# Half of a residual added by a gathering DMA, one bias addition moved to GpSimd, and two of eight steps with centre and gate in one matmul

## The chip, the core and the metric

The kernel runs on one core of a Trainium2 chip. Its time is the device time of one launch in microseconds; several runs are taken, and their median is the figure that counts. A profile is one further execution, recorded by the hardware profiler.

The engines are named as in the profile: PE is TensorE's matmul and PEld its weight load, DVE is VectorE, ACT is ScalarE, POOL is GpSimd, and SP is SyncE, which here only issues transfers. Each engine works through its own queue in order.

## The reference

The input `x` has 512 x 512 positions of 64 channels. Two layers are added to it, each to a group-normalized copy of its input:

```
x = x + L0(gn(x))            # triangle multiplication
x = x + L1(gn(x))            # 12 x 12 Fourier modes, mixed over channels
```

The first layer, cut to what matters here:

```
xn    = layernorm(x)
left  = (xn @ left_w + left_b)   * mask * sigmoid(xn @ lgate_w + lgate_b)
right = (xn @ right_w + right_b) * mask * sigmoid(xn @ rgate_w + rgate_b)
gate  = sigmoid(xn @ ogate_w + ogate_b)
out   = einsum('bkjd,bkid->bijd', left, right)
out   = layernorm(out) @ out_w + out_b
return out * gate
```

`mask` is 1 where both row and column are marked. About half of the 512 rows are, so `out` before the layernorm is zero at most positions.

## The kernel before

**Stages.** At most 256 rows are marked here, and the function `compact` packs these rows and columns. One after the other it takes statistics of `x` (to about 200 us of the profile), makes `left` and `right` (to 450), multiplies them channel by channel (to 620), computes `u` = layernorm(`out`) @ `out_w` + `out_b` for the marked positions (to about 750), runs the **output stage** (to about 1450) and, last, adds the Fourier layer and stores the result. The whole loop of the `u` steps and the output stage is one Python loop over steps `s`, which issues every engine's instructions in a hand-written order (`tc.manual_schedule`). The tile library adds only the waits between them.

**Steps and units.** Eight steps make a unit, `k, n = divmod(s, SIZE)`. The first 8 units are the `u` steps (`k < first`); the other 32 are the output stage, numbered `v = k - first`. A unit is a chunk of 32 columns times one half of the ranked rows. Its `x` is gathered as two transfers (`load`, r = 0 and 1) of 128 partitions x 32 positions x 64 channels, 1 MB each, into one of five buffers, `x_of(v)`, within the big tile `places`. For every second unit the rows are marked ones and `u` comes from memory by 32 transfers of `load_u`; for the others `u` is one constant row, `rows_of["out"]`.

**What a step does.** At step `s` the matmul engine transposes step `s + 13` (`t_ps`, line 1038), multiplies step `s` by the gate weights (`w_ps`, line 1045 through `times`) and step `s + 12` by the centring matrix (`c_ps`, the same line). ScalarE turns the transposed block into `xt_c` (line 1040), and squares the centred block (line 1076). VectorE sums the squares of two steps (line 1083), scales a step's gate product by the reciprocal root of the variance (line 1274) and, after each second step, adds the gate's bias to the part `z` of 16 positions (line 1280). A unit thus has four parts, c = 0 to 3. Each then goes through a sigmoid on ScalarE (line 1221), a product with `u` on GpSimd (`gated`, line 1109) and an addition to `x` on GpSimd (`added`, line 1113).

The root is taken once per unit, at step 5 of the unit before (`root`, line 1089). It needs another function table than the sigmoid, so two table loads stand around it.

**What is done with the sum.** `transform` (line 1140) multiplies the finished halves by a row basis: the half r = 0 at step 0 of the next unit, r = 1 at step 4. `statistics` (line 1168) takes VectorE's statistics of the finished unit four channel pairs a step, from step 3 of the next unit on. `store` writes a half to memory from SyncE: r = 0 at step 7 of its own unit, r = 1 at step 3 of the next. On the same queue `load_u` is issued at step 4 of each even unit. Every fourth unit the statistics are joined (`join_means`, `join_squares`, `join_rest`); after every second unit `save` copies the transform out of PSUM on ScalarE.

**Order within a unit, before.** Sigmoids stand at the even steps, products at the odd steps and additions at the even ones: part c has its sigmoid at step 2 + 2c, its product at 3 + 2c, its addition at 4 + 2c, counted on into the next unit. The gathers for unit `v + 3` stand behind the product at step 3 and behind the addition at step 6 on GpSimd's queue. PSUM holds two banks for `c_ps`, two for `w_ps`, two for `t_ps`, one for sums and biases (`scratch`) and one for the transform.

Of the kernel before, what the change touches and what calls it, by code (L numbers as in the profile page):

```python
# [9 lines left out]
F32 = mybir.dt.float32  # L10
# [36 lines left out]
def conv_preact_kernel(ctx: ExitStack, tc: tile.TileContext, t: dict):  # L47
# [573 lines left out]
    def compact(fc):  # L621
# [15 lines left out]
        def gather(dst, src, idx, r, jc):  # L637
            nc.gpsimd.indirect_dma_start(  # L638
                out=dst, out_offset=None, in_=src, in_offset=bass.IndirectOffsetOnAxis(ap=idx[:, r, jc : jc + 1], axis=0)
            )  # L640
# [190 lines left out]
        with tc.tile_pool(name="tri", bufs=1) as trp:  # L831
# [92 lines left out]
            with tc.manual_schedule(), tc.tile_pool(name="late", bufs=1) as lp:  # L924
# [65 lines left out]
                with tc.tile_pool(name="np_x", bufs=LEAD + 2) as tp, tc.tile_pool(name="np_q", bufs=2) as sqp, tc.tile_pool(  # L990
# [6 lines left out]
                    ps_c = ps_w = None  # L997

# [43 lines left out]
                    def times(pool, name, s, w):  # L1042
                        ps = pool.tile([P, 8, C], F32, name=name)
                        for i in range(4):
                            nc.tensor.matmul(ps[:, 2 * i : 2 * i + 2, :], xts[s][:, i, :], w, start=True, stop=True)  # L1045
                        return ps

                    def centered(s):
                        if s >= first * SIZE:
                            return times(ps_c, "c_ps", s, center_x)  # L1050

                        ps = ps_y.tile([P, 2, 4, P], F32, name="y_ps")
# [12 lines left out]

                    def of_pair(t, e):

                        return t.rearrange("p (h e i) c -> p h e i c", h=2, e=2)[:, :, e]

                    def squared(s, cps):  # L1070
                        n = s % SIZE
                        if n % 2 == 0:
                            sqs[s // 2] = sqp.tile([P, 16, C], F32, name="sq_c")
                        sq = sqs[s // 2][:, 8 * (n % 2) : 8 * (n % 2) + 8, :]
                        if s >= first * SIZE:
                            nc.scalar.activation(sq, cps, AF.Square)  # L1076
# [14 lines left out]
                    def load(k, r):  # L1091
                        jc, half = units[k]
                        gather(
                            x_of(k)[:, r * JC : (r + 1) * JC].rearrange("p j c -> p (j c)"), tiles, src_i, 2 * half + r, jc
                        )
# [6 lines left out]
                    def gated(k, c):  # L1102
# [6 lines left out]
                        nc.gpsimd.tensor_mul(zs[k, c], zs[k, c], u)  # L1109
# [5 lines left out]
                    def finished():  # L1115

                        z = zs.pop((last, 3))
                        made = [ps_c.tile([P, 8, C], F32, name="c_ps") for _ in range(2)]
# [74 lines left out]
                    for s in range(-LEAD, total_g + 2 * SIZE):  # L1193
# [12 lines left out]
                        if s + LEAD - 1 == first * SIZE:  # L1206
                            products.close()
                            ps_c = products.enter_context(tc.tile_pool(name="np_c", bufs=2, space=PSUM))
                            ps_w = products.enter_context(tc.tile_pool(name="np_w", bufs=2, space=PSUM))
                        if 0 <= s < total_g:  # L1210
                            wps = raw(s) if k < first else times(ps_w, "w_ps", s, gate_x)
                            del xts[s]
                        if 0 <= s + LEAD - 1 < total_g:
                            cps = centered(s + LEAD - 1)
                        if n in (0, 4) and held(1):
                            transform(v - 1, n // 4)

                        if n % 2 == 0:
                            i, c = (0, n // 2 - 1) if n >= 2 else (1, 3)
# [11 lines left out]
                        if n % 2 == 1:  # L1231
                            i, c = (0, (n - 3) // 2) if n >= 3 else (1, 3)
# [4 lines left out]
                        else:  # L1237
                            i, c = (0, (n - 4) // 2) if n >= 4 else (1, 2 + n // 2)
                            if held(i) and (v - i, c) != (last, 3):
                                added(v - i, c)  # L1240
# [21 lines left out]
                        if n == 7 and k + 1 in rss:  # L1262
                            nc.vector.reciprocal(factors[(k + 1) % 2] if k + 1 < first else rss[k + 1], rss[k + 1])
                        if wps is not None:
# [7 lines left out]
                            else:  # L1272
                                rs = rss[k][:, 8 * n : 8 * n + 8].unsqueeze(2).to_broadcast([P, 8, C])
                                nc.vector.tensor_mul(z[:, 8 * odd : 8 * odd + 8, :], wps, rs)  # L1274
                            if odd:
# [3 lines left out]
                                else:  # L1279
# [6 lines left out]
                                else:  # L1286
                                    zs[v, c] = z

                        if n == 7 and held(0) and v < last:
                            store(v, 0)  # L1290
# [243 lines left out]
```

## Time and profile before

| | |
|---|---|
| median of three runs | 1774.15 us (1771.41 to 1779.44) |
| the profiled execution, its own time | 1777.78 us |
| its span, first to last instruction | 1776.0 us |
| TensorE busy, share of the span | 1567.8 us, 88% |
| VectorE busy | 1413.7 us, 80% |
| ScalarE busy | 933.0 us, 53% |
| GpSimd busy | 936.5 us, 53% |
| moved by DMA | 518.48 MB, mean 292 GB/s |
| bias addition of the gate, VectorE, line 1280 | 128 of 1221 ns |
| scaling of the gate product, VectorE, line 1274 | 256 of 672 ns |
| product with `u`, GpSimd, line 1109 | 127 of about 2372 ns |
| addition to `x`, GpSimd, line 1113 | 127 of 2372 ns |
| gather of half a unit, GpSimd's issue, line 638 | 64 of 982 ns |

The shares are means over stages with different limits, so the output stage has to be read by itself. Busy times in the profile are unions of an engine's spans; instructions of one engine overlap a little, so the interval from one start to the next can be shorter than the duration. "Idle before, by X" in a row names the instruction whose end released the waiting one. A gather's landing time is counted from its issue on GpSimd to the arrival of its data.

### The profile page before, as it was taken

The page shows a single profiled execution, that of the slowest core. Times are in us where ns is not written, and L with a number is a line of the kernel's source. Part 1 is how long each engine was busy: PE and PEld are TensorE (multiplying, and loading weights), DVE is VectorE, ACT ScalarE, POOL GpSimd, SP SyncE. Part 2 cuts the span into 40 slices and gives each one's busy share as a digit, 9 for nine tenths or more (in the row PEclk, how much of TensorE's full clock was granted, in tenths as well). Part 3 has the DMA queues.
Part 4 walks back from the last instruction along what each step waited for, and adds up shares of the span by engine and source line. Part 5 has one row for each costly group of instructions (what it writes and reads, how often), then busy time and mean ns, then how long its engine had stood idle before and what let it go on. Part 6 is the DMA issues. An engine that isn't in the chain of part 4 may idle for free. (4 is left out here: it accounts for less than half of the span.)

```text
span 1776.0 us, 32619 instructions
## 1 busy us (share of the span) xinstructions
PE 1567.8 (88%) x10918; PEld 1242.0 (70%) x10918; DVE 1413.7 (80%) x2982; ACT 933.0 (53%) x1660; POOL 936.5 (53%) x695
## 2 busy tenths in 40 slices
PE   6779799997999978899999999999999977998772
PEld 5667666662899867787888888888888745665341
DVE  7989678887455568688999999999999984865451
ACT  3666566663333266676777777777777742011000
POOL 4666211111000037698999999999999881111110
PEclk9999999999899999899999999999999976555555
DMA  7999278878898789868767767776776699999999
GB/s 281 386 386 388 107 206 227 229 229 245 279 305 303 257 246 347 298 196 296 265 242 257 253 233 259 264 249 239 249 264 244 212 318 400 425 427 427 426 427 385
DMA packets 192593, 518.48 MB, mean 292 GB/s; under 512 B 37664, under 2 KB 104480, under 8 KB 151456
## 3 DMA queue, kind: packets, MB, share of 16 engines
q1 hardware_dynamic: 156112, 295.65, 47.5%
q0 software_dynamic: 32832, 218.45, 33.4%
q10 hardware_dynamic: 3472, 2.20, 0.5%
q8 instruction: 89, 1.46, 0.3%
q14 instruction: 88, 0.72, 0.1%
HBM read 311.60 MB, written 204.60 MB: 291 GB/s over the span
## 5 line engine op out<-in xcount | busy, mean ns | idle before, releaser
L1045 PE MATMUL w_ps<-gate_x,xt_c 128*128 128x128 f32 x2048 | 280.5, 281 | 30.0 <-DVE z_t L1274 28.6
L1113 POOL TENSOR_TENSOR places<-places,z_t 128x1024 f32<-128x1024 f32 x127 | 301.3, 2372 | 8.0
L1045 PEld LDWEIGHTS w_ps<-gate_x,xt_c 128*128 128x128 f32 x2048 | 252.0, 194 | 46.4 <-DVE z_t L1274 44.6
L1045 PE MATMUL c_ps<-center_x,xt_c 128*128 128x128 f32 x2048 | 277.0, 279 | 0.8 <-ACT xt_c L1040 0.4
L1045 PEld LDWEIGHTS c_ps<-center_x,xt_c 128*128 128x128 f32 x2048 | 252.8, 194 | 3.8 <-ACT xt_c L1040 3.0
L1440 PE MATMUL l_ps<-places,rinv 24*128 24x512 f32 x512 | 206.2, 1118 | 29.3 <-DVE places L1447 19.0
L1168 DVE BATCH_NORM_STATS2 stats2c<-places 128x6 f32<-128x128 f32 x1024 | 220.5, 278 | 9.9 <-POOL places L1113 9.9
L1083 DVE TENSOR_REDUCE scratch<-sq_c 128x16 f32<-128x1024 f32 x160 | 194.6, 1216 | 31.1 <-ACT sq_c L1078 16.1
L1221 ACT ACTIVATE z_t<-z_t 128x1024 f32<-128x1024 f32 x128 | 135.5, 1058 | 131.8 <-DVE z_t L1280 131.1
L1440 PEld LDWEIGHTS l_ps<-places,rinv 24*128 24x128 f32 x512 | 119.8, 302 | 110.8 <-DVE places L1447 56.9
L1278 POOL TENSOR_TENSOR z_t<-z_t,bias_row_out 128x1024 f32<-128x1024 f32 x32 | 75.6, 2363 | 226.3 <-PE y_ps L1058 202.1
L1040 ACT ACTIVATE xt_c<-t_ps,ab_xc 128x512 f32<-128x512 f32 x256 | 176.0, 688 | 11.5 <-PE t_ps L1038 10.6
L1274 DVE TENSOR_TENSOR z_t<-w_ps,rs_n 128x512 f32<-128x512 f32 x256 | 172.0, 672 | 6.2 <-PE w_ps L1045 6.1
L1076 ACT ACTIVATE sq_c<-c_ps 128x512 f32<-128x512 f32 x256 | 150.8, 589 | 31.4 <-PE c_ps L1045 30.8
L1280 DVE TENSOR_TENSOR z_t<-z_t,scratch 128x1024 f32<-128x1024 f32 x128 | 156.3, 1221 | 9.9 <-ACT rs_n L1089 3.7
L688 DVE BATCH_NORM_STATS2 stats1c<-x_ps 128x6 f32<-128x512 f32 x256 | 157.1, 682 | 7.7 <-PE x_ps L687 7.4
L1109 POOL TENSOR_TENSOR z_t<-z_t,places 128x1024 f32<-128x1024 f32 x64 | 151.8, 2371 | 14.6 <-ACT z_t L1221 14.4
L1038 PE MATMUL t_ps<-c_ident,places 128*128 128x128 f32 x1024 | 158.4, 278 | 0.0
L1038 PEld LDWEIGHTS t_ps<-c_ident,places 128*128 128x128 f32 x1024 | 118.5, 142 | 51.4 <-issue 51.4
L1447 DVE TENSOR_TENSOR places<-places,l_ps 128x512 f32<-128x512 f32 x176 | 109.3, 682 | 55.2 <-DMA places<-x_h,dst_i 42.1
L1109 POOL TENSOR_TENSOR z_t<-z_t,bias_row_out 128x1024 f32<-128x1024 f32 x63 | 149.4, 2372 | 5.8 <-ACT z_t L1221 5.5
L673 ACT COPY xc<-xg 128x128 f32 x352 | 105.0, 298 | 66.1 <-POOL xc L673 47.1
(214 smaller groups left out, 2557.0 us busy)
## 6 DMA issues: line engine op xcount, KB each, us to landing
x_h<-places SPq DMA_DIRECT2D x64, 1024.0 KB
out_x<-places SPq DMA_DIRECT2D x44, 1024.0 KB
places<-u_d SPq DMA_DIRECT2D x512, 64.0 KB
out_x<-lx_t SPq DMA_DIRECT2D x20, 1024.0 KB
rbc<-rs_d POOLq DMA_DIRECT2D x32, 512.0 KB, 7.1
left_d<-o_c SPq DMA_DIRECT2D x64, 256.0 KB
right_d<-o_c SPq DMA_DIRECT2D x64, 256.0 KB
left_raw<-left_d SPq DMA_DIRECT2D x64, 256.0 KB
```

Of the source, the lines that this page charges most:

```text
L688: nc.vector.bn_stats(stats[:, 0, 16 * (jc % quarter) + 4 * r + c, :], ps.rearrange("p i k -> p (i k)"))
L1038: nc.tensor.transpose(tps[:, i, :], flat[:, o : o + P], ident)
L1040: nc.scalar.activation(xts[s], tps, AF.Identity, bias=ab1[:, 2:3])
L1045: nc.tensor.matmul(ps[:, 2 * i : 2 * i + 2, :], xts[s][:, i, :], w, start=True, stop=True)
L1076: nc.scalar.activation(sq, cps, AF.Square)
L1083: nc.vector.tensor_reduce(totals[k % 2][:, 8 * (n - 1) : 8 * (n + 1)], sqs.pop(s // 2), AX.X, ALU.add)
L1109: nc.gpsimd.tensor_mul(zs[k, c], zs[k, c], u)
L1113: nc.gpsimd.tensor_add(xr, xr, zs.pop((k, c)))
L1168: nc.vector.bn_stats(st[k // 4][:, g, k % 4, :], x_of(k)[:, :, 2 * g : 2 * g + 2])
L1274: nc.vector.tensor_mul(z[:, 8 * odd : 8 * odd + 8, :], wps, rs)
L1280: nc.vector.tensor_add(z, z, bias_ps["ogate"].unsqueeze(1).to_broadcast([P, 16, C]))
L1440: nc.tensor.matmul(ps.rearrange("p j o -> p (j o)"), rinv[h, b, :], it[h], start=True, stop=True, tile_position=(32 * g, 0),)
```

## The change

Four things are changed in the output stage, and the order of the work is changed with them.

1. **Half of x by a second gather.** For parts 0 and 1 (the half r = 0) the product of gate and `u` is written over the unit's `x`, and at step 7 a gather of the same half of `x` is issued with an addition as its operation: it adds to what lies in SBUF. The additions of parts 0 and 1 on GpSimd go. The transform of this half moves from step 0 to step 2, and its store from step 7 to step 1 of the next unit.
2. **One bias addition on GpSimd.** Part 1 gets its bias by `biased` on GpSimd at step 4 instead of VectorE. Its sigmoid moves from step 4 to step 5, its product from step 5 to 6.
3. **Centre and gate as one matmul.** In steps with `s % 4 == 0`, eight matmuls with 64 rows multiply by `both`, which holds the 64 x 64 blocks of the centring and the gate matrix beside each other. ScalarE squares the one half of the result and copies the other into `xt_c`, from where VectorE scales it 12 steps later. Those steps take their factors from PSUM, so the reciprocal is made in two pieces.
4. **One PSUM pool.** Centre and gate products of a step share a tile of two banks from the pool that the `u` steps use; the pools `np_c` and `np_w` go.

```diff
-        def gather(dst, src, idx, r, jc):
+        def gather(dst, src, idx, r, jc, op=ALU.bypass):
             nc.gpsimd.indirect_dma_start(
...
+                compute_op=op,
             )
...
+                    def joint(s):
+
+                        return s >= first * SIZE and s % 4 == 0
+
+                    def times(bank, s, w):
                         for i in range(4):
-                            nc.tensor.matmul(ps[:, 2 * i : 2 * i + 2, :], xts[s][:, i, :], w, start=True, stop=True)
-                        return ps
...
+                            nc.tensor.matmul(bank[:, i, :], xts[s][:, i, :], w, start=True, stop=True)
+                        return bank.rearrange("p i (h c) -> p (i h) c", h=2)
+
+                    def centered(s, ps):
+                        if joint(s):
+                            for i in range(4):
+                                for h in range(2):
+                                    hs = slice(h * C, (h + 1) * C)
+                                    nc.tensor.matmul(ps[:, h, i, :], xts[s][hs, i, :], both[hs], start=True, stop=True)
+                            return ps
                         if s >= first * SIZE:
-                            return times(ps_c, "c_ps", s, center_x)
...
+                            return times(ps[:, 0], s, center_x)
...
-                        if s >= first * SIZE:
+                        if joint(s):
+                            nc.scalar.activation(in_order(sq), cps[:, :, :, :C], AF.Square)
+                            kept = xts[s].rearrange("p i (h c) -> p (i h) c", h=2)
+                            nc.scalar.copy(in_order(kept), cps[:, :, :, C:])
+                        elif s >= first * SIZE:
                             nc.scalar.activation(sq, cps, AF.Square)
...
-                        nc.gpsimd.tensor_mul(zs[k, c], zs[k, c], u)
+                        if c < 2:
+                            nc.gpsimd.tensor_mul(x_of(k)[:, 16 * c : 16 * c + 16, :], zs.pop((k, c)), u)
+                        else:
+                            nc.gpsimd.tensor_mul(zs[k, c], zs[k, c], u)
+
+                    def biased(k, c):
+                        bias = rows_of["ogate"].unsqueeze(1).to_broadcast([P, 16, C])
+                        nc.gpsimd.tensor_add(zs[k, c], zs[k, c], bias)
...
-                            products.close()
-                            ps_c = products.enter_context(tc.tile_pool(name="np_c", bufs=2, space=PSUM))
-                            ps_w = products.enter_context(tc.tile_pool(name="np_w", bufs=2, space=PSUM))
+                            for h in range(2):
+                                hs = slice(h * C, (h + 1) * C)
+                                nc.vector.tensor_copy(both[hs, :C], center_x[hs, hs])
+                                nc.vector.tensor_copy(both[hs, C:], gate_x[hs, hs])
+                        if s + LEAD - 1 >= 0 and s < total_g:
+                            ps = ps_y.tile([P, 2, 4, P], F32, name="y_ps")
                         if 0 <= s < total_g:
-                            wps = raw(s) if k < first else times(ps_w, "w_ps", s, gate_x)
-                            del xts[s]
+                            if k < first:
+                                wps = raw(s)
+                            elif joint(s):
+                                wps = xts[s].rearrange("p i (h c) -> p (i h) c", h=2)
+                            else:
+                                wps = times(ps[:, 1], s, gate_x)
                         if 0 <= s + LEAD - 1 < total_g:
-                            cps = centered(s + LEAD - 1)
-                        if n in (0, 4) and held(1):
+                            cps = centered(s + LEAD - 1, ps)
+                        if n in (2, 4) and held(1):
                             transform(v - 1, n // 4)
 
-                        if n % 2 == 0:
-                            i, c = (0, n // 2 - 1) if n >= 2 else (1, 3)
+                        if n in (0, 2, 5, 6):
+                            i, c = {0: (1, 3), 2: (0, 0), 5: (0, 1), 6: (0, 2)}[n]
                             if held(i):
                                 nc.scalar.activation(zs[v - i, c], zs[v - i, c], AF.Sigmoid)
...
-                        if n % 2 == 1:
-                            i, c = (0, (n - 3) // 2) if n >= 3 else (1, 3)
+                        if n == 7 and held(0):
+                            load(v, 0, ALU.add)
+                        if n in (1, 3, 6, 7):
+                            i, c = {1: (1, 3), 3: (0, 0), 6: (0, 1), 7: (0, 2)}[n]
                             if held(i) and (v - i, c) != (last, 3):
                                 gated(v - i, c)
                             elif held(i):
                                 finished()
-                        else:
-                            i, c = (0, (n - 4) // 2) if n >= 4 else (1, 2 + n // 2)
-                            if held(i) and (v - i, c) != (last, 3):
-                                added(v - i, c)
+                        if n == 4 and held(0):
+                            biased(v, 1)
+                        if n in (0, 2):
+                            c = 2 + n // 2
+                            if held(1) and (v - 1, c) != (last, 3):
+                                added(v - 1, c)
...
-                            nc.vector.reciprocal(factors[(k + 1) % 2] if k + 1 < first else rss[k + 1], rss[k + 1])
+                            if k + 1 < first:
+                                nc.vector.reciprocal(factors[(k + 1) % 2], rss[k + 1])
+                            else:
+                                by = [t.rearrange("p (a b) -> p a b", a=2) for t in (factors[(k + 1) % 2], rss[k + 1])]
+                                nc.vector.reciprocal(by[0][:, :, :8], by[1][:, :, :8])
+                                nc.vector.reciprocal(by[1][:, :, 8:], by[1][:, :, 8:])
...
-                                rs = rss[k][:, 8 * n : 8 * n + 8].unsqueeze(2).to_broadcast([P, 8, C])
+                                rs = (factors[k % 2] if joint(s) else rss[k])[:, 8 * n : 8 * n + 8]
+                                rs = rs.unsqueeze(2).to_broadcast([P, 8, C])
...
-                                else:
+                                elif c != 1:
                                     nc.vector.tensor_add(z, z, bias_ps["ogate"].unsqueeze(1).to_broadcast([P, 16, C]))
...
-                        if n == 7 and held(0) and v < last:
-                            store(v, 0)
+                        if n == 1 and held(1) and v - 1 < last:
+                            store(v - 1, 0)
```

More of the change, by code (lines that the diff above doesn't have):

```diff
@@ L635, in compact @@
         )
-        def gather(dst, src, idx, r, jc):
+        def gather(dst, src, idx, r, jc, op=ALU.bypass):
             nc.gpsimd.indirect_dma_start(
-                out=dst, out_offset=None, in_=src, in_offset=bass.IndirectOffsetOnAxis(ap=idx[:, r, jc : jc + 1], axis=0)
+                out=dst, out_offset=None, in_=src, in_offset=bass.IndirectOffsetOnAxis(ap=idx[:, r, jc : jc + 1], axis=0),
+                compute_op=op,
             )
@@ L996, in compact @@
                     ps_y = products.enter_context(tc.tile_pool(name="np_b", bufs=2, space=PSUM))
-                    ps_c = ps_w = None
                     both = lp.tile([P, P], F32, name="both")
@@ L1040, in transpose @@
                         nc.scalar.activation(xts[s], tps, AF.Identity, bias=ab1[:, 2:3])
-                    def times(pool, name, s, w):
-                        ps = pool.tile([P, 8, C], F32, name=name)
+                    def joint(s):
+                        return s >= first * SIZE and s % 4 == 0
+                    def times(bank, s, w):
                         for i in range(4):
-                            nc.tensor.matmul(ps[:, 2 * i : 2 * i + 2, :], xts[s][:, i, :], w, start=True, stop=True)
-                        return ps
-                    def centered(s):
+                            nc.tensor.matmul(bank[:, i, :], xts[s][:, i, :], w, start=True, stop=True)
[7 more added lines that the diff above has]
+                            return ps
                         if s >= first * SIZE:
-                            return times(ps_c, "c_ps", s, center_x)
-                        ps = ps_y.tile([P, 2, 4, P], F32, name="y_ps")
+                            return times(ps[:, 0], s, center_x)
                         q, e = divmod(s, 2)
@@ L1064, in raw, with in_order @@
                         return xts[s].rearrange("p h (i c) -> p (h i) c", c=C).rearrange("p (h i) c -> p h i c", h=2)
+                    def in_order(t):
+                        return t.rearrange("p (i h) c -> p h i c", h=2)
                     def of_pair(t, e):
@@ L1089, in root, with load @@
                         nc.scalar.activation(rss[k], totals[k % 2], AF.Sqrt, bias=eps, scale=1.0 / C)
-                    def load(k, r):
+                    def load(k, r, op=ALU.bypass):
                         jc, half = units[k]
                         gather(
-                            x_of(k)[:, r * JC : (r + 1) * JC].rearrange("p j c -> p (j c)"), tiles, src_i, 2 * half + r, jc
+                            x_of(k)[:, r * JC : (r + 1) * JC].rearrange("p j c -> p (j c)"), tiles, src_i, 2 * half + r, jc, op
                         )
@@ L1117, in finished @@
                         z = zs.pop((last, 3))
-                        made = [ps_c.tile([P, 8, C], F32, name="c_ps") for _ in range(2)]
+                        made = ps_y.tile([P, 2, 4, P], F32, name="y_ps")
+                        made = [made[:, i].rearrange("p i (h c) -> p (i h) c", h=2) for i in range(2)]
                         for i, ps in enumerate(made):
@@ L1287, in compact @@
                                     zs[v, c] = z
-                        if n == 7 and held(0) and v < last:
-                            store(v, 0)
+                        xts.pop(s, None)
+                        if n == 1 and held(1) and v - 1 < last:
+                            store(v - 1, 0)
                         if n == 3 and held(1) and v - 1 < last:
```

## Prediction, made before the changed kernel was run

> **What bounds the kernel now.** I read the busy shares first, then stretches of time, then one unit of the stage that is changed, engine by engine. The change touches only the output stage (32 units, each of 8 steps, after the u steps). In the answer for stretches the columns are stretch, length, busy time of TensorE, its weight load, VectorE, ScalarE and GpSimd, granted clock, DMA share and GB/s; it is followed by the answer for the gather's line, in the same stretch.
>
> ```profile
> 880.90:1317.10 436.20, 422.97 (x3571) 374.28 (x3570) 428.44 (x1008) 324.76 (x481) 416.34 (x201) 0.99 0.71 247
> 1485.90:1776.00 290.10, 224.92 (x608) 137.13 (x608) 158.91 (x256) 20.02 (x36) 46.00 (x49) 0.51 0.99 416
> ```
>
> ```profile
> L638 POOL DMA_INDIRECT places<-in_x,src_i x40: 977/984/988, 892.3 to 1314.3; - x40
> DMA to landing us min/median/max: 5.3/6.1/12.4
> ```
>
> The reader is to see that in the steady stretch three engines are full together: VectorE 98%, TensorE 97%, GpSimd 95%; ScalarE has 26% left, DMA 29%. Two gathers belong to a unit, so 40 of them are 20 units, and a unit takes 436.2 / 20 = 21.81 us. The last 290 us run at a DMA share of 0.99: they follow the output stage and shift with its end, so what a unit gains or loses is gained or lost in the total.
>
> Which of the three is hardest up is read in the timeline of one unit (start, duration, engine, line). GpSimd's rows from one gate product to the same one a unit later:
>
> ```profile
> 901.62 2.37 POOL L1109 TENSOR_TENSOR z_t<-z_t,bias_row_out 128x1024 f32<-128x1024 f32 x1
> 904.07 2.38 POOL L1113 TENSOR_TENSOR places<-places,z_t 128x1024 f32<-128x1024 f32 x1
> 906.39 2.37 POOL L1109 TENSOR_TENSOR z_t<-z_t,bias_row_out 128x1024 f32<-128x1024 f32 x1
> ...
> 911.17 2.37 POOL L1109 TENSOR_TENSOR z_t<-z_t,places 128x1024 f32<-128x1024 f32 x1
> 913.68 0.99 POOL L638 DMA_INDIRECT places<-in_x,src_i  x1
> 914.69 2.38 POOL L1113 TENSOR_TENSOR places<-places,z_t 128x1024 f32<-128x1024 f32 x1
> ...
> 921.99 0.98 POOL L638 DMA_INDIRECT places<-in_x,src_i  x1
> 922.99 2.38 POOL L1109 TENSOR_TENSOR z_t<-z_t,places 128x1024 f32<-128x1024 f32 x1
> ```
>
> Eight vector instructions and two gathers fill 922.99 - 901.62 = 21.37 us, and none shows a wait. VectorE's unit (one reciprocal to the next, 901.92 to 922.89) is 20.97 us with 20.76 busy. GpSimd thus falls back 0.4 us in such a unit and catches up in each fourth one, where VectorE joins statistics: L1173, L1174, L230, L1185 and L1186 add about 2.3 us of rows. A cut must come off both engines, and must bring no wait onto either.
>
> **The change, part by part.** *VectorE* loses one bias addition of four per unit (L1280, 1.22 us, in the timeline 1.14 from its start to the next start). Its reciprocal of 64 values (0.54 us) becomes two, of 16 and 48. Between a cost that grows with the values (+0.1) and a full second one (+0.45) I take +0.2, since rows of 32 values (190 ns) show a floor. Two of eight scalings read SBUF in place of PSUM, as L1271 does in the u steps (684 against 672 ns): nothing. Net -0.94: 20.0 us in a plain unit, 20.7 as a mean with the joins.
>
> *TensorE.* A centre or gate step costs 0.89 us each between starts. The u steps show the joint form (L1058): 30 records in 2.05 us, so 16 in 1.09. Two steps of eight save 1.78 - 1.09, 1.4 us per unit. TensorE's rows of a plain unit are 8 steps of 2.22 us and two transforms of 1.0, about 20; it falls to 18.5. That is not the bound; if VectorE and GpSimd were faster, it would be worth its 1.4.
>
> *ScalarE* gets two copies of 0.59 us (L1079's duration), 1.2 per unit: 15.9 to 17.1 of 21.8. They lie at the even steps 0 and 4, not in the chain below.
>
> *GpSimd* loses two of four additions of x (L1113) and gains one bias addition: seven vector instructions. It gains a third gather, with an addition, whose issue I take at the 0.98 us of the present ones (nothing nearer; up to 2 us if it needs a second set of descriptors).
>
> The order matters more than the sum. Each unit now has gate product 0, a gather, the bias addition for part 1, and *nothing* until ScalarE has taken the sigmoid of that part; then gate product 1, a gather, the adding gather, gate product 2. From starts in the rows: product 0 to gather 2.51; gather 1.01; bias addition 2.37, which ends at 5.89. Behind the sigmoid of part 1 on ScalarE's queue stand the square root with its own table, a square, a bias copy, the table back, and the sigmoid of part 2, for which gate product 2 waits. Rows of ScalarE that give these intervals:
>
> ```profile
> 904.35 1.06 ACT L1221 ACTIVATE z_t<-z_t 128x1024 f32<-128x1024 f32 x1 [0.93 <-DVE z_t L1280]
> ...
> 916.04 0.68 ACT L1040 ACTIVATE xt_c<-t_ps,ab_xc 128x512 f32<-128x512 f32 x1
> 916.74 1.28 ACT L1089 ACT_TABLE_LOAD   x1
> 918.03 0.31 ACT L1089 ACTIVATE rs_n<-scratch,eps 128x64 f32<-128x64 f32 x1
> 918.24 0.59 ACT L1076 ACTIVATE sq_c<-c_ps 128x512 f32<-128x512 f32 x1
> 918.72 0.69 ACT L1040 ACTIVATE xt_c<-t_ps,ab_xc 128x512 f32<-128x512 f32 x1
> 919.78 1.28 ACT L1221 ACT_TABLE_LOAD   x1 [0.36 <-DVE z_t L1280]
> 921.07 1.06 ACT L1221 ACTIVATE z_t<-z_t 128x1024 f32<-128x1024 f32 x1
> ```
>
> Wake-up after VectorE's bias addition 0.09 (904.35 against 903.04 + 1.22), taken for GpSimd too; sigmoid 1.08; table 1.29; root 0.21; square 0.48; copy 0.70; table 1.29; sigmoid 1.06: 6.11. Gate product 2 starts at 5.89 + 0.09 + 6.11 + 0.1 = 12.19. GpSimd's own way there (sigmoid 1.27 with wake-ups, product 1 2.51, two gathers 2.02) reaches only 11.69, so ScalarE's chain decides by 0.5 us. Then product 2, addition 2, product 3, addition 3: 2.45 + 2.32 + 2.45 + 2.32 = 9.54, and the next unit starts at 21.73. In each second unit the save of the transform (L1148, 0.59) lies in the chain: 22.23. Additions 2 and 3 now follow directly on the product they read; a gather that does so today starts 0.15 late, so up to 0.1 more for each. Mean: 22.1. Against 21.81 this is +0.29 per unit, 9 us over 32. In the first six units (748 to 881, 22.2 us each) other waits are in the way; I count them alike.
>
> Here a rule of the Trainium skill is weighed: "ScalarE: Activation LUTs", What ACT_TABLE_LOAD costs, gives a load of 1283 ns and a drain of about 1380 ns for every switch. The rows have 1.28 us and the next instruction 0.01 later, and the load starts 0.02 after the work before. With the drain twice in the chain a unit would be 24.9 us, +98 us in all; by the rows it is 22.1, and I go by the rows.
>
> *The adding gather's landing* is the new wait of a transfer. It is issued at 5.89 + 1.27 + 2.51 + 1.01 = 10.7 us of the unit, straight behind the gather for a later unit. Behind it wait the transform's first half (moved to step 2, TensorE), the statistics from step 3 (VectorE), and the store of the half (moved to step 1, SyncE; behind that the second store and the loads of u, which have steps to spare). In today's trace the transform of step 4 starts 4.0 us after gate product 0 (1023.44 against 1019.40), so that of step 2 about 0.4 before it: the budget is 22.1 - 0.4 - 10.7 = 11.0 us. The gather ahead needs 6.1 - 1.0 = 5.1 more. A MB on this queue costs 33.4% of 1776 us / 218.45 MB = 2.7 us, a half unit of 1.05 MB 2.85 us. Landing is then 8.0 us, within the budget. The Trainium skill's "Collectives: The Full Stack", The bandwidth ceiling: the fold count and why AG ≠ RS ≠ AR, says why an add in the DMA takes twice as long: two reads per chunk on the ring (ratio 1.93). By that rule, which no row here shows, it is 10.6 us, at the budget's edge, and the DMA share of the stage goes from 0.71 to 0.96 instead of 0.84. Behind a gather that takes 12.4 us, as some do today, it would be late by 6 us (3 by the row). I estimate a quarter late by 5 us: 1.2 us per unit, 40 us in all. Ends 0 and +40; I take +3, nearer to the row.
>
> Removing the change of PSUM pools before the first unit saves under 1 us; filling the joint weights there (four copies) costs as much. Sum: 9 + 3 = +12 us on the profiled execution, whose own time is 1777.78 us (1776.0 span, 1.8 around it): 1790. The median, 3.6 us lower, goes to **1786 us**, 0.7% slower. Half a percent, 9 us, is about what a measurement can tell from no change.
>
> **Rivals.** *GpSimd alone sets the pace (faster).* If ScalarE's chain is shorter than its present intervals make it, gate product 2 starts at 11.69 and a unit is 11.69 + 9.54 = 21.2 to 21.4: -0.4 to -0.6, over 32 units -13 to -19 us, 1755 to 1761. For it: VectorE and TensorE do get lighter, and its joins no longer show. Against it: the order of ScalarE's queue is fixed. It decides from 11.9 us on. A fall below 21.2 is excluded by seven instructions of 2.37, three issues and one exposed sigmoid.
>
> *The adding gather is late (much slower).* At twice the DMA time it comes after its budget; TensorE stops at the transform, and with it scalings, bias addition and the next adding gather. 1.2 us per unit gives 1774 + 9 + 40 = 1823; all units late by 2 us 1850. For it: share 0.96, landings to 12.4. Against it: DMA has 29% free, and the landing by the row is 8.0.
>
> *No effect:* waits move between three full engines and the unit stays at 21.8: 1774.
>
> **How the numbers follow.** ScalarE's chain 0.50, with its own range 1776 to 1796, a third of it under 1783; GpSimd alone 0.17; late gather 0.25; no effect 0.08. Faster 0.17; same 0.17 + 0.08 = 0.25; slower 0.33 + 0.25 = 0.58. The range 1762 to 1825 leaves out the best of the second case and the worst of the third.
>
> **What would show it.** A bias addition on GpSimd with an idle of about 1.2 us ahead of gate product 1, released by the sigmoid, and a smaller one ahead of product 2; a steady unit of 22.1 us; VectorE near 92% and TensorE near 90% busy, both waiting; the adding gather landing in 8 to 10 us and hardly any wait of the transform for it. A unit under 21.5 or waits on the adding gather of over 1 us each would prove it wrong.

## The result, and the profile after

The changed kernel takes **1907.16 us** (median of four runs, 1899.87 to 1908.51); the kernel before, run beside it, 1776.8 us. The ratio is 1.0729 (1.0688 to 1.077): 130 us slower, where the prediction had 12 us slower and a range to 1825. In one sentence: the unit of the output stage has become 25.8 us long in place of 21.8, because one transfer lands later than its place in the unit allows, and behind that wait other new waits lie hidden.

The page of the changed kernel: its span, the queue of the gathers, the chain that ended last by engine, and three groups of instructions.

```profile
span 1906.2 us, 32563 instructions
...
q0 software_dynamic: 37440, 252.00, 40.4%
...
DMA 25%; PE 17%; DVE 5%; POOL 5%; issue 4%; ACT 2%; SPq 2%; POOLq 0%; DVEq 0%; ACTq 0%
...
L1314 DVE TENSOR_TENSOR z_t<-y_ps,rs_n 128x512 f32<-128x512 f32 x192 | 129.6, 675 | 146.1 <-ACT sq_c L1091 142.6
...
L1163 PE MATMUL f_ps<-places,hb 128*32 128x512 f32 x512 | 75.6, 665 | 94.8 <-DMA places<-in_x,src_i 80.6
...
L638 POOL DMA_INDIRECT places<-in_x,src_i x96 | 113.4, 1181 | 27.9 <-issue 10.4
```

Two groups have idle time ahead of them that they did not have: the scaling of the gate product (line 1314) waits 142.6 us in all for ScalarE's square, and the transform (line 1163) 80.6 us for a gather. The queue of the gathers has moved 33.55 MB more than the 218.45 MB it had before and shows what an addition costs there: 40.4% of 1906.2 us against 33.4% of 1776.0 us is 177 us of all 16 engines, 5.3 us for a MB, where the old gathers took 2.7.

The steady stretch (columns as in the prediction: busy time of TensorE, weight load, VectorE, ScalarE, GpSimd, clock, DMA share, GB/s), and in it GpSimd's bias addition, of which each unit has one:

```profile
985.10:1450.20 465.10, 372.61 (x3219) 313.88 (x3218) 373.03 (x910) 313.37 (x470) 361.83 (x181) 0.96 0.84 254
```

```profile
L1131 POOL TENSOR_TENSOR z_t<-z_t,bias_row_ogate x21: 2367/2376/2423, 946.5 to 1463.1; 128x1024 f32<-128x1024 f32 x21
```

No engine is full any more: TensorE and VectorE are at 80%, GpSimd at 78%, DMA at 84%. The 21 bias additions start 20 units apart, (1463.1 - 946.5) / 20 = 25.83 us. Against 21.81 this is 4.0 us a unit, 129 us over 32 units: all of the loss is here.

One unit, from the timeline of the engines (start, duration, engine, line, idle time before and its end); the lines are put in order of time, each from the answer for its engine. The landing is that of the gather at 1060.99.

```profile
1060.99 1.58 POOL L638 DMA_INDIRECT places<-in_x,src_i  x1 [0.30 <-issue]
...
1080.03 2.37 POOL L1131 TENSOR_TENSOR z_t<-z_t,bias_row_ogate 128x1024 f32<-128x1024 f32 x1 [2.87 <-DVE z_t L1314]
1083.57 2.36 POOL L1125 TENSOR_TENSOR places<-z_t,bias_row_out 128x1024 f32<-128x1024 f32 x1 [1.17 <-ACT z_t L1251]
1086.07 0.96 POOL L638 DMA_INDIRECT places<-in_x,src_i  x1
1087.34 1.58 POOL L638 DMA_INDIRECT places<-in_x,src_i  x1 [0.30 <-issue]
```

```profile
DMA to landing us min/median/max: 12.4/12.4/12.4
```

```profile
1073.52 1.06 PE L1163 MATMUL f_ps<-places,hb 128*32 128x512 f32 x8 [2.22 <-DMA places<-in_x,src_i]
...
1075.40 1.92 PE L1047 MATMUL y_ps<-gate_x,xt_c 128*128 128x128 f32 x8
1077.11 1.49 PE L1047 MATMUL y_ps<-center_x,xt_c 128*128 128x128 f32 x8
...
1081.54 1.06 PE L1047 MATMUL y_ps<-gate_x,xt_c 128*128 128x128 f32 x8
```

```profile
1078.63 0.60 ACT L1091 ACTIVATE sq_c<-y_ps 128x512 f32<-128x512 f32 x1 [2.30 <-PE y_ps L1047]
...
1082.43 1.06 ACT L1251 ACTIVATE z_t<-z_t 128x1024 f32<-128x1024 f32 x1
```

```profile
1079.26 0.69 DVE L1314 TENSOR_TENSOR z_t<-y_ps,rs_n 128x512 f32<-128x512 f32 x1 [3.51 <-ACT sq_c L1091]
```

This is a circle. The adding gather is issued at 1060.99 and lands at 1073.4; the transform, held 2.22 us, runs at 1073.52, and TensorE's products for part 1 of the next unit come after it. Their scaling waits 3.51 us for the square of its step; the bias addition, the sigmoid, gate product 1 and a plain gather follow, and at 1087.34 the next adding gather is issued. Landing 12.4 and the way from there to the next issue 13.9 make 26.35 us, and that is the length of this unit. Every step of it starts within 0.3 us of the end of the one before, so lateness is not made up: what the landing takes too long, each unit takes longer.

The way back has a second cost in it, in the clock. The first row is the 3.42 us behind the transform in this unit, the second as long a stretch from the transform's start in the next (columns as above):

```profile
1074.58:1078.00 3.42, 3.42 (x18) 3.42 (x18) 1.17 (x5) 0.69 (x1) 2.43 (x2) 0.50 1.02 419
1099.40:1102.82 3.42, 3.42 (x30) 2.58 (x31) 3.28 (x6) 1.49 (x3) 2.88 (x2) 1.00 0.41 115
```

At the granted clock of 0.50 the gate products at 1075.40 took 1.92 us, and at 1.00 those at 1081.54 took 1.06. From the transform's start to the next adding gather it is 12.2 us in the median of 14 units with the full clock and 13.8 in that of ten units with such a stretch (the 24 units whose adding gathers are issued from 879.5 to 1470.4 us). Nine of these ten follow a wait of the transform of 2.2 us or more. An estimate from these figures: 1.6 us in 10 of 24 units are 21 us over 32, at most, because the kernel before has such stretches too (17 us in all between 950 and 1420 us, here 34). No run takes this part by itself.

### The profile page after: what moved, and what is told of

It reads as the page before. It is cut to its first block, busy times and chain, and to the rows that moved or that the text cites. A ratio compares the mean times of both kernels' runs of the same rounds, so it can differ in the third digit from the quotient of the medians.

```text
span 1906.2 us, 32563 instructions
## 1 busy us (share of the span) xinstructions
PE 1547.3 (81%) x10918; PEld 1202.7 (63%) x10918; DVE 1388.9 (73%) x2986; ACT 969.4 (51%) x1724; POOL 913.6 (48%) x695
## 3 DMA queue, kind: packets, MB, share of 16 engines
q0 software_dynamic: 37440, 252.00, 40.4%
## 4 chain that ended last, share of the span: by engine, by line
DMA 25%; PE 17%; DVE 5%; POOL 5%; issue 4%; ACT 2%; SPq 2%; POOLq 0%; DVEq 0%; ACTq 0%
DMA places<-in_x,src_i 15%; PE y_ps L1047 6%; DMA out_x<-places 4%; PE l_ps L1481 4%; PE f_ps L1163 2%; PE t_ps L1037 2%; DMA out_x<-lx_t 2%; DMA places<-x_h,dst_i 2%; POOL places L638 2%; POOL z_t L1131 1%; DMA places<-u_d 1%; DVE stats2c L1191 1%; DVE z_t L1314 1%; PE y_ps L1055 1%; SPq L647 1%
## 5 line engine op out<-in xcount | busy, mean ns | idle before, releaser
L1047 PE MATMUL y_ps<-gate_x,xt_c 128*128 128x128 f32 x1536 | 224.9, 293 | 47.7 <-DVE z_t L1314 24.9
L1047 PEld LDWEIGHTS y_ps<-gate_x,xt_c 128*128 128x128 f32 x1536 | 199.2, 203 | 71.6 <-DVE z_t L1314 39.1
L1314 DVE TENSOR_TENSOR z_t<-y_ps,rs_n 128x512 f32<-128x512 f32 x192 | 129.6, 675 | 146.1 <-ACT sq_c L1091 142.6
L1098 DVE TENSOR_REDUCE scratch<-sq_c 128x16 f32<-128x1024 f32 x160 | 194.5, 1216 | 26.8 <-ACT sq_c L1093 12.2
L1047 PE MATMUL y_ps<-center_x,xt_c 128*128 128x128 f32 x1536 | 208.7, 280 | 0.0
L1047 PEld LDWEIGHTS y_ps<-center_x,xt_c 128*128 128x128 f32 x1536 | 193.0, 197 | 0.6 <-ACT xt_c L1039 0.2
L1318 POOL TENSOR_TENSOR z_t<-z_t,bias_row_out 128x1024 f32<-128x1024 f32 x32 | 75.6, 2363 | 225.9 <-PE y_ps L1065 202.3
L1163 PE MATMUL f_ps<-places,hb 128*32 128x512 f32 x512 | 75.6, 665 | 94.8 <-DMA places<-in_x,src_i 80.6
L1135 POOL TENSOR_TENSOR places<-places,z_t 128x1024 f32<-128x1024 f32 x63 | 148.8, 2362 | 4.9
L1091 ACT ACTIVATE sq_c<-y_ps 128x512 f32<-128x512 f32 x192 | 113.7, 592 | 47.5 <-PE y_ps L1047 47.4
L638 POOL DMA_INDIRECT places<-in_x,src_i x96 | 113.4, 1181 | 27.9 <-issue 10.4
```

Source lines behind the costliest of these rows:

```text
L638: nc.gpsimd.indirect_dma_start(out=dst, out_offset=None, in_=src, in_offset=bass.IndirectOffsetOnAxis(ap=idx[:, r, jc : jc + 1], axis=0), ...
L1047: nc.tensor.matmul(bank[:, i, :], xts[s][:, i, :], w, start=True, stop=True)
L1098: nc.vector.tensor_reduce(totals[k % 2][:, 8 * (n - 1) : 8 * (n + 1)], sqs.pop(s // 2), AX.X, ALU.add)
L1135: nc.gpsimd.tensor_add(xr, xr, zs.pop((k, c)))
```

## The experiments

**Theories.** *Landing*: the circle through the adding gather alone sets the unit. *Shared tile*: product and centre of a step now lie in one PSUM tile, and the tile library puts the two engines that read it in order, so that the scaling of step s waits for ScalarE's square of the same tile, though it needs none of its data. *Chain*: the sigmoids that GpSimd waits for, as predicted. The kernel before was run beside each group (medians 1778.6 to 1781.4); "+67" below is against that run's own median. Lines are from the stretch 950 to 1420 us. In the diffs "-" is the kernel named in the heading. Chains of waits give: engine and line, waited for, total us, times, longest.

**The changed kernel with separate PSUM tiles.**

```diff
-    ps = ps_y.tile([P, 2, 4, P], F32, name="y_ps")
+    ps[0] = ps_c.tile([P, 4, P], F32, name="c_ps")
+    ps[1] = ps_w.tile([P, 4, P], F32, name="w_ps")
```

> The changed kernel with centre and gate products in separate PSUM tiles again (a joint step takes one of each; its square and its copy become two instructions each). The new thing tried is the wait of the gate scaling on the square of the same step, which came with the shared tile. Theory L+S (the adding gather's landing closes a cycle: transform of step 2, gate product, scaling, bias addition, sigmoid, product, gather, adding gather; the shared tile lengthens it by one centre product, one transposed copy and one square): the cycle shortens by 1.6 to 2.0 us per unit, 1907 falls to 1843 to 1856. Theory L alone (only the landing counts, scaling is not in the chain): 1900 to 1910. Theory S alone (the shared tile is the whole loss): back to 1775 to 1795.

1904.21 us (1899.92 to 1911.95), ratio 1.0694 (1.0663 to 1.0725), +126, as expected of the landing alone. The scaling no longer waits for the square, and nothing is gained that the intervals can tell. The landing is enough to hold the unit at 25.8 us.

**The changed kernel with a plain gather in place of the adding one.**

```diff
-    load(v, 0, ALU.add)
+    load(v, 0, ALU.bypass)
```

> The changed kernel with the second gather as a plain one: it overwrites the half, so gate times u is left out of that half of x. Transfer, issue and waits stay; the addition in the DMA goes. Theory L+S[...]: landing falls from about 12 to 8 or 9 us and issue from 1.58 to 1.0 us, the cycle by 3 to 4 us, until GpSimd and ScalarE set the pace at 21.5 to 22.5: 1780 to 1810. Rival (the extra megabyte and the order count, not the addition): 1890 to 1910.

1845.72 us (1842.23 to 1846.96), ratio 1.0370 (1.0342 to 1.0399), +67. This kernel leaves gate times `u` out of that half. The same packets without the addition give half of the loss back, not all: a time between the two expectations. What is left:

```profile
DVE z_t L1314 <- ACT sq_c L1091: 53.2, 23, 3.7
...
PE f_ps L1163 <- DMA places<-in_x,src_i: 1.7, 3, 0.7
```

The transform waits no more, the scaling does. The second holder was under the first; each undone alone shows little or half.

**The kernel before with the shared tile only.**

```diff
-    wps = raw(s) if k < first else times(ps_w, "w_ps", s, gate_x)
+    wps = raw(s) if k < first else times(ps[:, 1], s, gate_x)
...
-    cps = centered(s + LEAD - 1)
+    cps = centered(s + LEAD - 1, ps)
```

> The kernel before with only the shared PSUM tile of two banks for centre and gate products (no adding gather, no joint matmul, bias additions on VectorE). The scaling then waits for the square of its step. Theory L+S: without a landing in the chain the wait costs VectorE, which is full, what the square comes later than the gate product: 0 to 1 us per unit, 1775 to 1805. Rival S alone (the shared tile is the loss by itself): 1850 to 1905.

1865.73 us (1863.57 to 1867.45), ratio 1.0485 (1.0458 to 1.0512), **+87**, for an edit that adds no instruction and no byte. It is the rival's range. VectorE, which waited 2.1 us in all for its products in this stretch before, now waits for the square, and TensorE waits longer for the scaling than its 14.6 us before:

```profile
DVE z_t L1271 <- ACT sq_c L1074: 54.5, 47, 1.5
PE y_ps L1044 <- DVE z_t L1271: 51.5, 36, 2.3
```

Two rows of ScalarE and one of VectorE show how:

```profile
1011.94 0.31 ACT L1087 ACTIVATE rs_n<-scratch,eps 128x64 f32<-128x64 f32 x1
1012.15 0.59 ACT L1074 ACTIVATE sq_c<-y_ps 128x512 f32<-128x512 f32 x1
```

```profile
1012.77 0.69 DVE L1271 TENSOR_TENSOR z_t<-y_ps,rs_n 128x512 f32<-128x512 f32 x1 [1.08 <-ACT sq_c L1074]
```

The square stands behind a table load and the root on ScalarE's queue; the scaling, which before waited only for its product, starts when it ends.

**The same with the square issued behind the scaling.** Between the two places stands VectorE's work of the step, with the scaling.

```diff
-    if cps is not None:
-        squared(s + LEAD - 1, cps)
...
+    if cps is not None:
+        squared(s + LEAD - 1, cps)
```

> The kernel before with the shared two-bank tile (1866 by itself), and ScalarE's square of the later step issued behind VectorE's scaling in the step, nothing else. If the 87 us of the shared tile come from the scaling being held until the square of the same tile is done, the order of two engines' reads, they go: 1775 to 1800. If they come from the two banks being handed back together, with only two such pairs for TensorE to write, the order of the reads matters little: 1850 to 1870.

1830.20 us (1820.79 to 1832.16), ratio 1.026 (1.022 to 1.0301), +49: between both expectations. The wait turned round:

```profile
ACT sq_c L1074 <- DVE z_t L1269: 118.8, 93, 3.3
PEld y_ps L1044 <- ACT sq_c L1074: 54.7, 55, 2.5
```

Now the square waits for the scaling, the root behind it comes later, and TensorE waits for the square before it may write the pair of banks again. So the other order of the reads takes 38 of the 87 us away: the scaling's wait has gone and the square's has come. The rest is the square's wait and the late return of the two banks together, which this run does not separate.

**The changed kernel with both undone** (separate tiles and a plain gather: the first two diffs together).

> The changed kernel with both suspects undone at once: product and centre in separate PSUM tiles, and a plain gather in place of the adding one (that half of the output holds the tile gathered again, without gate times u). If the late landing and the shared tile are all of the loss, and only overlapped, what is left is the GpSimd and ScalarE chain of the prediction, 22.1 us a unit against 21.8: 1780 to 1800. If the chain of sigmoids ahead of GpSimd's products is a third loss that the other two covered, the plain-gather run's 1846 hardly moves: 1830 to 1850.

1829.61 us (1822.99 to 1830.84), ratio 1.0264 (1.0229 to 1.03), +48. The expectation of 1780 to 1800 failed. Counted from one reciprocal to the next, 17 of 22 units are 21.8 to 23.2 us long, but five stand out with 24.7 to 28.9. In these the transform waits 2.1 to 6.5 us, in four of them, by the profile, for the gather:

```profile
PE f_ps L1166 <- DMA places<-in_x,src_i: 19.2, 10, 6.5
```

**Separate tiles and no second gather.**

```diff
-    if n == 7 and held(0):
-        load(v, 0, ALU.add)
```

> The changed kernel with separate PSUM tiles and no second gather at all: half of the output holds gate times u without x, so what is left of the change is the joint matmuls, the bias addition on GpSimd and the moved sigmoids and products. With a plain gather in its place it was 1830, of which five late units in 22 made about 33 us and a base unit of 22.4 us (21.8 before) the rest. If the base unit is that chain, the prediction's third loss: 1790 to 1800. If the GpSimd issue and the gather's packets cost nothing but the late units are ScalarE's own backlog and stay: 1815 to 1830.

1795.05 us (1791.66 to 1797.13), ratio 1.0083 (1.0054 to 1.0113), **+15.5**, as the first expectation had it. What is left is the chain, and one part of it that I had not seen:

```profile
POOL z_t L1130 <- ACT z_t L1265: 38.4, 21, 2.1
DVE z_t L1332 <- ACT rs_n L1107: 32.6, 20, 2.2
POOL places L1128 <- ACT z_t L1265: 28.7, 32, 1.2
```

```profile
L1134 POOL TENSOR_TENSOR z_t<-z_t,bias_row_ogate x22: 2364/2374/2390, 947.0 to 1416.3; 128x1024 f32<-128x1024 f32 x22
```

This kernel leaves `x` out of that half. GpSimd waits for the sigmoids ahead of products 1 and 2, as predicted (1.8 us a time ahead of product 2, where 0.5 was foretold with the adding gather's issue, 1.0 us, in the same gap), and the unit is (1416.3 - 947.0) / 21 = 22.35 us (22.1 predicted). VectorE waits 1.6 us a time for the root as well: its bias addition reads the bias from `scratch`, the PSUM tile from which the root reads its totals, and the root now stands behind a sigmoid that waits for GpSimd.

**The adding gather with neither TensorE nor VectorE to wait for it** (separate tiles). The modes and statistics are then those of other data.

```diff
-    x_of(k)[:, o : o + 8, :].rearrange("p j c -> p (j c)"),
+    x_of(k - 1 if k and r == 0 else k)[:, o : o + 8, :].rearrange("p j c -> p (j c)"),
...
-    nc.vector.bn_stats(st[k // 4][:, g, k % 4, :], x_of(k)[:, :, 2 * g : 2 * g + 2])
+    xs = x_of(k)[:, JC:, 2 * g : 2 * g + 2].unsqueeze(1).to_broadcast([P, 2, JC, 2])
+    nc.vector.bn_stats(st[k // 4][:, g, k % 4, :], xs)
```

> The changed kernel with separate PSUM tiles (1904 by itself) and the adding gather kept, but nothing on TensorE or VectorE reads the half that it writes: the transform of that half reads the same half of the unit before, and the statistics read the other half twice; only its store still waits for it. The modes and statistics of the output stage are therefore of other data. If it is the landing that is waited for, the time falls to that of the run with a plain gather and separate tiles, within 15 us, whatever that is. If it is the traffic (the queues' share was 0.84 to 0.90 with the adding gather) that delays the other loads and slows the rest, it stays above that run by 40 us or more.

1853.73 us (1848.49 to 1861.99), ratio 1.0424 (1.0387 to 1.0461), +72. It lies 24 us above the run with a plain gather, between the two expectations: of the 77 us that the addition costs with separate tiles (+126 against +48), 53 are the wait for its landing, the low clock behind it included. The other 24 are there although nothing of a unit waits for the half. What the addition still brings is the longer time in the queue and the longer issue (1.58 against 0.94 us), and a gather waits here for a store as well:

```profile
POOL places L638 <- DMA x_h<-places: 13.3, 3, 10.6
```

How the 24 divide between these was not tried.

**One load issued later.** The adding gather stands on its queue 1.3 us behind a plain gather of the same size (1 MB, not half of one, as the expectation has it), the second half for the unit three ahead. Here that one goes to step 1 of the next unit (separate tiles).

```diff
-    if n == 6:
-        load(v + 3, 1)
+if n == 1 and 0 <= v + 2 < len(units):
+    load(v + 2, 1)
```

> The changed kernel with separate PSUM tiles (1904) and its adding gather, but the plain gather that was issued 1.3 us ahead of it on the same queue (second half of the unit three ahead) is issued three steps later. If the adding gather lands late (11.6 to 15.5 us) because it stands behind that half megabyte in the queue, it now lands in 7 to 9 us, the transform hardly waits, and the time falls to that of the run in which nobody read the half: 1840 to 1865. If it is late because the addition itself makes every packet take longer, it stays at 11 us or more and the time at 1890 to 1910.

1856.96 us (1839.47 to 1859.75), ratio 1.0405 (1.0349 to 1.046), +78: the time of the run in which nobody read the half. The waits of the transform with the load ahead (first) and later (second):

```profile
PE f_ps L1166 <- DMA places<-in_x,src_i: 62.5, 17, 8.9
```

```profile
PE f_ps L1166 <- DMA places<-in_x,src_i: 25.6, 11, 5.1
```

Between 980 and 1450 us the eleven adding gathers whose landing is recorded take 8.9 to 12.9 us, median 9.4; with the load ahead 17 take 10.8 to 17.6, median 11.8. But the move does two things. The landing is shorter, and the load's issue no longer stands in the way back:

```profile
1062.40 2.36 POOL L1128 TENSOR_TENSOR places<-z_t,bias_row_out 128x1024 f32<-128x1024 f32 x1 [2.15 <-ACT z_t L1265]
1065.03 1.58 POOL L638 DMA_INDIRECT places<-in_x,src_i  x1 [0.27 <-POOL places L1128]
```

From gate product 1 to the adding gather it is 2.63 us, against 1087.34 - 1083.57 = 3.77 in the rows of the changed kernel. The two together are worth 48 us; they were not separated.

**The same move with a plain second gather.**

> The same move of one load in the run with separate tiles and a plain second gather (1830; it leaves out gate times u in that half). Without any second gather it was 1795. If its 35 us are the place in the queue behind the load: 1795 to 1812, what is left being one more issue on GpSimd. If they are the 1.05 MB more of traffic in a unit: 1820 to 1835.

1819.22 us (1818.09 to 1820.63), ratio 1.0228 (1.0209 to 1.0247), +40. No unit is late for a gather any more (0.5 us of wait in the stretch), but this is 8 us below the run without the move (+40 against +48) and not 33: a unit without a late gather has become (1431.1 - 948.1) / 21 = 23.0 us. The load's issue, 0.98 us, now stands ahead of the bias addition in GpSimd's chain, and VectorE's wait for the root has grown from 30.1 to 46.5 us. Both expectations are missed by a little: the late units go with the load ahead, and the move has its own price.

**The changed kernel with that move alone** (tile still shared).

> The changed kernel (1907) with that one load issued three steps later and nothing else, so product and centre still share a PSUM tile. With separate tiles the same move gave 1857. If the late landing alone sets the time of the changed kernel, as the separate tiles' gain of only 3 us suggested: 1855 to 1865. If the shared tile is a second holder of nearly the same length, hidden under the landing: 1870 to 1895.

1871.51 us (1861.68 to 1876.52), ratio 1.0513 (1.046 to 1.0565), +92. One moved load takes 38 of the 130 us away, though the median of the 11 recorded landings falls only from 11.9 to 11.1 us, and now the shared tile, worth 3 to 5 us before, is worth 14.5:

```profile
DVE z_t L1314 <- ACT sq_c L1091: 68.9, 26, 5.6
...
PE f_ps L1163 <- DMA places<-in_x,src_i: 17.0, 8, 3.9
```

**Two parts alone in the kernel before.** The adding gather for parts 0 and 1, issued at step 6, with transform and store moved as in the change:

```diff
-    nc.gpsimd.tensor_mul(zs[k, c], zs[k, c], u)
+    if c < 2:
+        nc.gpsimd.tensor_mul(x_of(k)[:, 16 * c : 16 * c + 16, :], zs.pop((k, c)), u)
+    else:
+        nc.gpsimd.tensor_mul(zs[k, c], zs[k, c], u)
...
+    if n == 6 and held(0):
+        load(v, 0, ALU.add)
```

> The kernel before with the adding gather alone: no bias addition on GpSimd, no joint matmul, separate PSUM tiles, sigmoids and products at their old steps; the adding gather is issued at step 6 behind product 1 of step 5, transform of the half at step 2, store at step 1. Theory L+S: from landing to the next adding gather the chain is about 8.2 us here (no bias addition on GpSimd, no square in it), with a landing of 12 us 20.2, under VectorE's 21 us, so the landing is covered: 1765 to 1785, GpSimd with 3 us idle per unit. Rival (DMA crowded out by a transfer that counts double): loads and stores come late whatever the order, 1820 to 1880.

1843.74 us (1839.75 to 1846.57), ratio 1.0362 (1.0331 to 1.0393), +65, in the range of the rival, although GpSimd loses two additions of 2.37 us a unit.

```profile
950.00:1420.00 470.00, 432.87 (x3638) 384.43 (x3631) 435.56 (x1024) 329.08 (x486) 358.41 (x183) 0.98 0.90 284
```

GpSimd is at 76% and VectorE at 93%; the DMA share is 0.90. GpSimd's relief brings nothing: VectorE was as full, and the transform waits for landings (21.3 us, 7 times). That is not all of the 65 us; what the rest is was not tried.

The joint matmuls alone, with separate tiles, a second reciprocal and everything else as before:

```diff
+    if joint(s):
+        for i in range(4):
+            for h in range(2):
+                hs = slice(h * C, (h + 1) * C)
+                nc.tensor.matmul(ps[h][:, i, :], xts[s][hs, i, :], both[hs], start=True, stop=True)
+        return ps
```

> The kernel before with the joint matmuls of two steps in eight alone (separate PSUM tiles, so their square and their copy are two instructions each). TensorE gets shorter and ScalarE about 2.4 us a unit longer, VectorE 0.2 us for the second reciprocal. If VectorE and GpSimd alone set the unit as the prediction had it: 1778 to 1792. If ScalarE's extra instructions hold back the sigmoids or the root for GpSimd and VectorE: 1800 to 1830.

1791.68 us (1791.46 to 1792.19), ratio 1.0069 (1.0043 to 1.0095), +12. TensorE's 1.4 us a unit are worth nothing; the price is at the upper end of what the second reciprocal and ScalarE's extra instructions were to cost. This was the smallest loss of the parts that were tried alone (the bias addition on GpSimd was not), and no version here beats the kernel before.

The losses as one staircase, each step against the one before: chain and joint matmuls 15.5; a plain second gather behind a load 33; the addition in it, apart from the wait for its landing, 24; by that wait 53; the shared tile on top 5. Together 130. The order matters: the parts overlap, and taken alone the shared tile is the largest.

## Why the prediction was wrong

**VectorE and TensorE: right.** The two reciprocals take 0.24 and 0.40 us, the joint step 1.16; neither engine is the bound, at 80% each.

**ScalarE's chain: right, and its size a little low.** Unit 22.35 us against 22.1, +15.5 us against +9. The waits of GpSimd ahead of products 1 and 2 are those foretold; VectorE's wait for the root, through `scratch`, was not in it. How much of the 15.5 is the joint matmuls' (12 by themselves) was not separated.

**"I take +3, nearer to the row": the step that failed.** It is three mis-sizings of one mechanism, which the text had in its second rival with a chance of 0.25 and 40 us. First the landing: 8.0 us was put together from the row of plain gathers that stand alone, 6.1, and 2.85 us for the half unit. The changed kernel's landings are 10.8 to 17.4, median 11.9. The rule of the Trainium skill that was set against the row ("Collectives: The Full Stack", The bandwidth ceiling: the fold count and why AG ≠ RS ≠ AR: two reads for an add, hence 10.6) came nearer: 5.3 us for a MB here against 2.7. The row measured another operation. The page speaks of the add in a ring of ranks, though, and no run shows that a second read is the reason here. Second the budget: 11.0 us was the place of the transform in a unit of 22.1 us in which nothing else moves. What counts is how long the way is from the landing to the next adding gather. In the unit above it took 13.9 us, which leaves 7.9 for a unit of 21.8; with the full clock it takes 12.3, which leaves 9.5. Third the form: I priced lateness as an accident of a quarter of the units. In a circle every unit is as long as its landing and that way together.

So the term that stood at +3 measures 110 of the 130 us: 33 for a plain gather in that place, 24 and 53 for the addition. The load ahead of it is a part of this: its move takes 48 us away with separate tiles and 38 as the kernel stands.

**"Removing the change of PSUM pools ... saves under 1 us": wrong too.** I looked at the one moment at which pools change, and not at who shares a tile afterwards. By itself the shared tile costs 87 us; in the changed kernel 5 when the landing covers it, 14.5 when the load is moved, 19 with a plain gather (+67 against +48). Why it costs so much less there is open. Fewer scalings that wait (six of eight) and VectorE's lighter unit may be the reason; neither was tried.

**The sign that was named came.** "Waits on the adding gather of over 1 us each would prove it wrong": there are 17 in the stretch, 43.8 us, 2.6 each.

## What to carry to other kernels

When a transfer becomes part of a unit's own loop of work (issued late in it, needed early in the next), price it as a circle: its landing, with what stands ahead of it on its queue, plus the whole way from the landing back to its next issue; compare the sum with the unit. Before two engines' data go into one tile, list who reads each tile, because the library may order reads that have nothing to do with each other. And when one suspect is undone and nothing is gained, undo the second with it before the first is acquitted: here 5 and 63 us alone became 82 together.

## What the runs showed of the hardware

An indirect gather with an addition takes GpSimd 1.58 us to issue in place of 0.98, and its share of the queue rises by 5.3 us for a MB. The plain second gather of the same 33.55 MB raised it by 2.4 (37.1% of a span of 1827.1 us against 33.2% of 1794.4). When the plain gather of the same size, issued 1.3 us ahead of the adding one, went elsewhere, the median landing of the adding one fell from 11.8 to 9.4 us with separate tiles and from 11.9 to 11.1 with the shared one (11 to 17 recorded landings in each run). In the changed kernel the granted clock was 0.50 in stretches of 3.4 to 10.2 us, mostly behind a wait of TensorE for the landing, and eight matmuls took 1.92 us in such a stretch in place of 1.06.
